# First norm of a four-layer graph kernel: steps in a written order, the mean taken away by a product, small weights loaded by GpSimd, idle products ahead of the input

## The chip, the cores and the metric

The kernel runs on one core of a Trainium2 chip. The metric is the device time of one execution in microseconds (us); lower is better. A core has a matrix engine (TensorE, "PE" in the profile, its weight loads are "PEld"), a vector engine (VectorE, DVE), a scalar engine (ScalarE, ACT), GpSimd (POOL) and a queue engine (SyncE, SP). Each works through its own instructions in the order in which they stand in its queue, and waits at an instruction until the semaphores that it needs have come. Transfers between memory and the on-chip buffers are DMAs; here they are issued by SP or by GpSimd.

## What is computed

`x` has 8 batches of 2048 nodes with 64 features. Four graph layers follow each other, and each has the form x = x + layer(relu(layernorm(x))):

```python
def _layernorm(x, axis=-1, eps=1e-5):
    m = jnp.mean(x, axis=axis, keepdims=True)
    v = jnp.var(x, axis=axis, keepdims=True)
    return (x - m) / jnp.sqrt(v + eps)
...
    h = jnp.maximum(_layernorm(x, axis=-1), 0.0)
    x = x + _L0_gnn_ref(h, L0_gnn_H, adj, 64, L0_gnn_W, L0_gnn_W_ind, ...)
```

The change lies in the first of these norms and in what is done beside it. Layer 0 uses the normed `h` in two ways. The first is a neighbourhood mean, `industry = einsum('nm,bmf->bnf', adj / deg, x @ W_ind)` (with x standing for h). The second is an attention over the members of 64 groups given by the 2048 x 64 matrix `H`. For that second part the kernel makes lists of (node, group) pairs from H.

## The kernel before

**Layout.** Two batches lie on the 128 partitions (2 x 64 features), so there are four pairs p of batches, and the 2048 nodes lie along the free dimension. The input comes transposed as `xT` [4, 128, 2048]. A half is 1024 nodes of one pair: 8 halves in all, each a 512 KB tile `x`, loaded in two parts of 256 KB. A mean over 64 features is a product with `avg`, a block-diagonal 128 x 128 matrix of 1/64, so that each feature's partition gets the mean of its own batch.

**The first stage (lines 882 to 912).** For each half: `mean = avg @ x` on TensorE (two products of 512 columns), `xc = x - mean` on DVE, `q = xc^2` on ScalarE, `var = avg @ q` on TensorE, `q = exp(-0.5 ln(var + eps))` on ScalarE in two instructions, and `hn = max(xc, 0) * q` on DVE. The helper `norm` (line 757) runs the steps of `norm_steps` (line 739) one after the other. Then eight products of 128 columns with `W_ind` give two tiles `py` (line 902); ScalarE copies them, rounded, to `Y[0]`, and DVE writes the rest `py - Y[0]` to `Y[1]` (lines 904 and 905).

**Beside the norm.** After the first pair `pairs` (line 833) makes the lists: it loads `H` as `M` (twice, line 844) and its transpose `MT` (line 847), counts with products against the triangle matrix `tri` (tiles `pr` and `pc`) and does DVE work that ends in `Q`, `mid`, `width` and the flags `bad`. After the second pair `weights` (line 813) and `layer1_weights` (line 684) load and multiply small weights, after the third `layer2_weights` (line 699). All these loads are issued by SP, 37 of them with `W_ind`, most of 64 x 64 or 64 x 1 elements.

**What sets the order.** The program text is not the order of the instructions. A scheduling layer places them on the engines, and a tile pool makes a new tile wait until the tile that had its place is released. Only instructions handed to `keep_in_program_order` keep the order of the text; the class `InOrder` (line 622) does that for all instructions of an engine that are issued through it, and `Kit.mm` (line 724) does it for products while `kit.strict` is set. In the first stage none of this was used. In that stage's PSUM pool `mean` has one place, `var` two and `yy` (py, pr, pc and the small products) two.

**What follows.** The second stage (line 914) streams the transposed adjacency in tiles `at` of 512 KB, six places, issued by GpSimd (line 932), and adds `Y` products into four sums `acc` (line 940); between these stand the products `ph` (line 982) and the other work of `members`. The `at` tiles and the sums lie where tiles of the first stage lay. SP also issues three copies of the input from memory to memory (`xd`, line 1241), and the loads `bw`, which wait for the first stage's places.

Of the kernel before, what the change touches and what calls it, by code (L numbers as in the profile page):

```python
# [16 lines left out]
P = 128  # L17
B, N, F = 8, 2048, 64
E = 64
# [615 lines left out]
class Kit:  # L635


    def __init__(self, tc, t, pool):
# [8 lines left out]
        for b2 in range(2):  # L647
            nc.vector.memset(self.avg[half(b2), half(b2)], 1.0 / F)
        self.eps = pool.tile([P, 1], FP, name="eps_f")
# [28 lines left out]
    def block_diag_in(self, w, src):  # L678
        self.nc.vector.memset(w, 0.0)
        for b2 in range(2):  # L680
            self.nc.sync.dma_start(out=w[half(b2), half(b2)], in_=src)
        return w

    def layer1_weights(self, pool, ps):
# [6 lines left out]
        for b2 in range(2):  # L691
            nc.sync.dma_start(out=a4[half(b2), b2 : b2 + 1], in_=t["L1_gnn_a"][F : 2 * F, :])
            nc.sync.dma_start(out=a4[half(b2), 2 + b2 : 3 + b2], in_=t["L1_gnn_a"][0:F, :])
        nc.vector.tensor_copy(self.W1x[:, 0:P], W)
        pw = ps.tile([P, 4], FP, tag="yy", name="pw1")
        nc.tensor.matmul(pw, WT, a4, start=True, stop=True)
        nc.vector.tensor_copy(self.W1x[:, P : P + 4], pw)

    def layer2_weights(self, pool, ps):

        nc, t, mm = self.nc, self.t, self.nc.tensor.matmul
# [4 lines left out]
        for dst, src in ((self.b1, "b1"), (self.b2c, "b2"), (self.ivc, "intervention_value")):  # L706
            for b2 in range(2):
                nc.sync.dma_start(out=dst[half(b2), :], in_=t[f"L2_gnn_{src}"])

        for dst, w in ((self.Wvc, self.W1v), (self.Wec, self.W1e)):  # L710
            pw = ps.tile([P, P], FP, tag="yy", name="pw2")
            mm(pw, W2n, w, start=True, stop=True)
            nc.vector.tensor_copy(dst, pw)
        pw = ps.tile([P, 1], FP, tag="yy", name="pwc")
        mm(pw, self.W1v, self.b2c, start=True, stop=True)
        nc.vector.tensor_add(self.b1c, pw, self.b1)
        r = pool.tile([P, P], FP, name="b2r")
        for h in range(2):
            nc.vector.tensor_scalar(r[:, half(h)], self.ones, self.b2c, None, op0=OP.mult)
        pw = ps.tile([P, P], FP, tag="yy", name="pwb")  # L720
        mm(pw, r, self.W1e, start=True, stop=True)
        nc.vector.tensor_copy(self.cb, pw)
# [33 lines left out]

    def norm(self, *tiles):
        for _ in self.norm_steps(*tiles):
            pass


def layer0(kit, hn, x1_dram, open_early, late_tile, between):
# [40 lines left out]
    with ExitStack() as sA:  # L803
# [9 lines left out]
        def weights(pool, ps):  # L813
# [5 lines left out]
            for b2 in range(2):  # L819
                nc.sync.dma_start(out=a2[half(b2), b2 : b2 + 1], in_=t["L0_gnn_a_node"])  # L820
                nc.sync.dma_start(out=a2[half(b2), 2 + b2 : 3 + b2], in_=t["L0_gnn_a_gn"])
            nc.sync.dma_start(out=a_ge, in_=t["L0_gnn_a_ge"].rearrange("f o -> o f").to_broadcast([P, F]))
            nc.sync.dma_start(out=fcb, in_=t["L0_gnn_fcb"])
            nc.sync.dma_start(out=av, in_=t["L0_gnn_av"])
            for b2 in range(2):
                nc.sync.dma_start(out=fcW[half(b2), :], in_=t["L0_gnn_fcW"])
            nc.vector.tensor_scalar(Av, ones, av, None, op0=OP.mult)
            nc.vector.tensor_copy(Wx[:, 0:P], W)
            pw = ps.tile([P, 4], FP, tag="yy", name="pw")
            mm(pw, WT, a2, start=True, stop=True)  # L830
            nc.vector.tensor_copy(Wx[:, P : P + 4], pw)

        def pairs(pool, ps):
# [4 lines left out]
            nc.vector.tensor_copy(slot, tmp)  # L838
# [1237 lines left out]
```

## Time and profile before

| | us |
|---|---|
| median of 3 runs | 2058.82 |
| lowest and highest of them | 2055.77, 2061.78 |
| the profiled execution: its own time | 2053.27 |
| its span in the profile | 2051.2 |
| first product of the first stage starts | 4.45 |
| first `acc` product of the second stage starts | 69.51 |
| end of the first eight `acc` and the first two `ph` products | 72.03 |
| mean granted TensorE clock over the span | 0.989 |

In the timeline each row has a start, a length, the engine, the line of the code, the operation and `out<-in`; in brackets stands how long the engine was idle before it and what ended that. SPq and POOL rows with `DMA_DIRECT2D` are the issue of a transfer, not the transfer. The releasers are inferred from semaphores. A product of fp32 data shows as two records of TensorE, so a count of x4 is two products. A granted clock of 1.00 is the full TensorE clock.

### The profile page before, as it was taken

The page shows a single profiled execution, that of the slowest core. Times are in us where ns is not written, and L with a number is a line of the kernel's source. Part 1 is how long each engine was busy: PE and PEld are TensorE (multiplying, and loading weights), DVE is VectorE, ACT ScalarE, POOL GpSimd, SP SyncE. Part 2 cuts the span into 40 slices and gives each one's busy share as a digit, 9 for nine tenths or more (in the row PEclk, how much of TensorE's full clock was granted, in tenths as well). Part 3 has the DMA queues.
Part 4 walks back from the last instruction along what each step waited for, and adds up shares of the span by engine and source line. Part 5 has one row for each costly group of instructions (what it writes and reads, how often), then busy time and mean ns, then how long its engine had stood idle before and what let it go on. Part 6 is the DMA issues. An engine that isn't in the chain of part 4 may idle for free.

```text
span 2051.2 us, 23618 instructions
## 1 busy us (share of the span) xinstructions
PE 1992.0 (97%) x9164; PEld 1153.7 (56%) x9164; DVE 1184.3 (58%) x1867; ACT 454.4 (22%) x859; POOL 291.4 (14%) x399
## 2 busy tenths in 40 slices
PE   7999899988999999999999999999999999999997
PEld 4777677623323232237774567665477745677653
DVE  6667399866888888873216552245622165522355
ACT  4321255474111111121120111211111211112100
POOL 0211187511000000000001110101100011101012
PEclk9999899999999999999999999999999999999998
DMA  6766173185011111204101012100021001121000
GB/s 172 207 192 189 59 249 113 36 228 107 27 47 37 47 32 42 52 11 111 57 21 29 24 42 67 47 15 24 23 68 57 21 22 30 42 67 46 8 15 12
DMA packets 84251, 138.17 MB, mean 67 GB/s; under 512 B 32752, under 2 KB 33008, under 8 KB 81456
## 3 DMA queue, kind: packets, MB, share of 16 engines
q1 hardware_dynamic: 65200, 83.86, 13.9%
q0 software_dynamic: 18928, 52.70, 10.5%
q8 instruction: 74, 1.21, 0.3%
q14 instruction: 49, 0.40, 0.1%
HBM read 102.64 MB, written 37.03 MB: 68 GB/s over the span
## 4 chain that ended last, share of the span: by engine, by line
PE 71%; issue 15%; POOL 4%; DVE 3%; DMA 3%; ACT 2%; SPq 0%; POOLq 0%; DVEq 0%; ACTq 0%
PE acc L726 28%; PE o L726 11%; PE dn L726 6%; PE u L726 6%; PE pd L726 3%; PE acc L940 3%; PE pgs L726 2%; PE var L726 2%; PE mean L726 2%; PE py L726 2%; POOL fold L1964 1%; DMA iv<-ind_dram 1%; PE pm L726 1%; POOL ot L1965 1%; PE ph L726 1%
## 5 line engine op out<-in xcount | busy, mean ns | idle before, releaser
L726 PE MATMUL acc<-aT,parts 128*128 128x512 f32 x1664 | 456.0, 419 | 0.0
L726 PEld LDWEIGHTS acc<-aT,parts 128*128 128x128 f32 x1664 | 307.8, 188 | 111.8 <-issue 49.4
L1952 DVE TENSOR_TENSOR pr<-u,embf 128x512 f32<-128x512 f32 x256 | 170.6, 687 | 139.0 <-PE u L726 132.3
L1571 DVE SCALAR_TENSOR_TENSOR pt<-R,wd,aT 128x1024 f32<-128x1024 f32 x192 | 236.3, 1277 | 18.4 <-PE dn L726 6.6
L726 PE MATMUL u<-W3f,y 64*128 64x512 f32 x1024 | 241.0, 589 | 0.0
L726 PE MATMUL o<-pt,hS 128*64 128x512 f32 x1024 | 236.4, 599 | 0.8 <-DVE pt L1571 0.6
L726 PEld LDWEIGHTS u<-W3f,y 64*128 64x128 f32 x1024 | 99.2, 187 | 120.6 <-issue 120.6
L726 PEld LDWEIGHTS o<-pt,hS 128*64 128x64 f32 x1024 | 68.0, 136 | 159.2 <-issue 150.2
L726 PE MATMUL u<-W3f,v 64*128 64x512 f32 x512 | 138.8, 619 | 0.0
L940 PE MATMUL acc<-at,Y 128*128 128x512 f32 x512 | 134.9, 408 | 1.7 <-DVE ev L949 1.7
L1964 POOL TENSOR_TENSOR fold<-fold 128x256 f32<-128x256 f32 x64 | 47.8, 747 | 548.2 <-DVE fold L1963 510.4
L726 PE MATMUL dn<-pt,vd 128*32 128x512 f32 x1024 | 123.1, 598 | 0.0
L1788 DVE TENSOR_TENSOR yb<-py,cb_f 128x512 f32<-128x512 f32 x32 | 22.1, 691 | 173.8 <-PE py L726 173.8
L940 PEld LDWEIGHTS acc<-at,Y 128*128 128x128 f32 x512 | 94.2, 192 | 24.8 <-issue 4.1
L726 PE MATMUL acc<-aTl,parts 128*128 128x512 f32 x384 | 103.1, 405 | 0.0
L1956 DVE TENSOR_TENSOR pr<-pr 128x512 f32<-128x512 f32 x128 | 88.1, 688 | 2.2
L1571 DVE SCALAR_TENSOR_TENSOR pt<-R,wd,aTl 128x1024 f32<-128x1024 f32 x64 | 79.8, 1281 | 11.4 <-PE dn L726 8.2
L726 PEld LDWEIGHTS acc<-aTl,parts 128*128 128x128 f32 x384 | 72.2, 188 | 21.5 <-issue 5.7
L1856 POOL TENSOR_TENSOR bq<-bq,xp 128x512 f32<-128x512 f32 x16 | 20.6, 1285 | 434.0 <-DVE xp L1854 395.1
L1938 ACT COPY xs<-px 128x128 f32<-128x128 f32 x64 | 17.1, 267 | 272.7 <-POOL ot L1966 210.2
L630 POOL TENSOR_TENSOR mix<-ex,wt 128x512 f32<-128x512 f32 x64 | 68.3, 1069 | 33.7 <-DVE ex L630 28.9
L726 PEld LDWEIGHTS dn<-pt,vd 128*32 128x32 f32 x1024 | 26.7, 108 | 80.8 <-issue 75.4
(322 smaller groups left out, 2723.0 us busy)
## 6 DMA issues: line engine op xcount, KB each, us to landing
at<-in_adjT POOLq DMA_DIRECT2D x32, 512.0 KB, 4.5
raw<-in_adjT SPq DMA_DIRECT2D x64, 256.0 KB, 3.3
aT<-in_adjT POOLq DMA_DIRECT2D x12, 1024.0 KB, 5.3
xp<-xd SPq DMA_DIRECT2D x45, 256.0 KB, 3.2
R<-r_dram SPq DMA_DIRECT2D x14, 512.0 KB, 3.7
hi_dram<-hi SPq DMA_DIRECT2D x16, 264.0 KB, 2.5
lo_dram<-lo SPq DMA_DIRECT2D x16, 264.0 KB, 3.4
hhi<-hi_dram POOLq DMA_DIRECT2D x16, 264.0 KB, 3.1
```

The costliest lines, as they stand in the source:

```text
L630: self.tc.keep_in_program_order(getattr(self.engine, name)(*args, **kw))
L726: one = self.nc.tensor.matmul(*args, **kw)
L940: mm(acc[p], Y[h][:, m, p, :], at[:, k, :], start=m + h == 0, stop=m == NT - 1 and h == 1)
L1571: nc.vector.scalar_tensor_tensor(pt, R[b2], wd[:, m, b2 : b2 + 1], aT[m][:, s].bitcast(FP), op0=OP.max, op1=OP.mult)
L1788: nc.vector.tensor_tensor(yb, py, bias[:, None, :].to_broadcast([P, 4, P]), op=OP.add)
L1856: nc.gpsimd.tensor_add(bq, bq, xp)
L1938: nc.scalar.copy(xs.rearrange("p h f -> p (h f)"), px)
L1952: nc.vector.tensor_tensor(a, u[h], emb[:, i, 8 * w : 8 * w + 8, None].to_broadcast([P, 8, F]), op=OP.mult)
L1956: nc.vector.tensor_add(pr[h], pr[h], a)
L1964: nc.gpsimd.tensor_add(fold[:, :, 0:2, :], fold[:, :, 0:2, :], fold[:, :, 2:4, :])
L1965: nc.gpsimd.tensor_add(ot, fold[:, :, 0, :], fold[:, :, 1, :])
```

## The change

- A matrix `cen = ident - avg` is made. `xc` is now the product `cen @ x` and stays in PSUM (two places); DVE's subtraction is gone, and Square and the last DVE instruction read PSUM. `var` has one place.
- The stage is written as steps: in step i TensorE gets var of half i-1, xc of half i and the map py of half i-2, with everything on TensorE, DVE and ScalarE kept in the text's order (`kit.strict`, `V`, `A`). The parts of `pairs` are spread over steps 0 to 7.
- The 37 small loads are issued by GpSimd. Their DVE copies stand in step 5, their products and the copies of these in step 8, in one PSUM tile.
- Six products of `avg` with `avg` go to a tile that nobody reads, ahead of the first x.
- On SP the order becomes: the first three x, MT, M twice, x of the fourth and fifth half, two of the three `xd` copies, the sixth x, the third copy, and the last two x.
- In the second stage the four sums of the first columns are allocated ahead of `pg` and `pd`. In the built program the first two `ph` products stand ahead of the first `acc` product; before they stood behind eight of them. They wait for the last `Y[1]` subtraction. From the first members of the second stage on, each engine's instructions stand in the same order as before.

```diff
+        self.cen = pool.tile([P, P], FP, name="cen_f")
+        nc.vector.tensor_sub(self.cen, self.ident, self.avg)
...
     def block_diag_in(self, w, src):
         self.nc.vector.memset(w, 0.0)
         for b2 in range(2):
-            self.nc.sync.dma_start(out=w[half(b2), half(b2)], in_=src)
+            self.nc.gpsimd.dma_start(out=w[half(b2), half(b2)], in_=src)
...
-    def layer2_weights(self, pool, ps):
+    def layer2_weights(self, pool, V, pw):
...
+                nc.gpsimd.dma_start(out=dst[half(b2), :], in_=t[f"L2_gnn_{src}"])
         r = pool.tile([P, P], FP, name="b2r")
+        yield
         for h in range(2):
-            nc.vector.tensor_scalar(r[:, half(h)], self.ones, self.b2c, None, op0=OP.mult)
+            V.tensor_scalar(r[:, half(h)], self.ones, self.b2c, None, op0=OP.mult)
+        yield
...
-            for p in range(NP):
-                for hf in range(2):
-                    s = cols(hf, HN)
-                    x = sb.tile([P, HN], FP, tag="x", name="x", bufs=3)
-                    for k in range(2):
-                        nc.sync.dma_start(out=x[:, cols(k)], in_=t["xT"][p, :, cols(2 * hf + k)])
-                    mean = ps.tile([P, HN], FP, tag="mean", name="mean", bufs=1)
-                    var = ps.tile([P, HN], FP, tag="var", name="var")
-                    xc = sb.tile([P, HN], FP, tag="xc", name="xc")
-                    q = sb.tile([P, HN], FP, tag="q", name="q")
-                    kit.norm(hn[p][:, s], x, mean, var, xc, q)
...
+            def centred(i):
+                x = xs.pop(i)
+                xc = xcs[i] = ps.tile([P, HN], FP, tag="xc", name="xc")
+                for k in range(2):
+                    kit.mm(xc[:, cols(k)], kit.cen, x[:, cols(k)], start=True, stop=True)
+
+            def squared(i):
+                q = qs[i] = sb.tile([P, HN], FP, tag="q", name="q")
+                A.activation(q, xcs[i], AF.Square)
...
+            def scaled(i):
+                p, hf = halves[i]
+                q = qs.pop(i)
+                A.activation(q, vs.pop(i), AF.Ln, bias=kit.eps)
+                A.activation(q, q, AF.Exp, scale=-0.5)
+                V.scalar_tensor_tensor(hn[p][:, cols(hf, HN)], xcs.pop(i), 0.0, q, op0=OP.max, op1=OP.mult)
...
+            def places():
+
+                all_ = ps.tile([P, 2 * CW], FP, tag="xc", name="pw")
+                at = iter(range(0, 2 * CW, P))
+                return lambda n: (lambda a: all_[:, a : a + n])(next(at))
+
+            fetched(0)
+            fetched(1)
+
+            idle = ps.tile([P, HN], FP, tag="var", name="idle", bufs=1)
+            for k in range(6):
+                nc.tensor.matmul(idle[:, 0:P], kit.avg, kit.avg, start=True, stop=True)
+            listed = pairs(pool, ps, V)
+            small = [f(pool, V, lambda n: pw(n)) for f in (weights, kit.layer1_weights, kit.layer2_weights)]
+            kit.strict = True
+            n = len(halves)
+            for i in range(n + 2):
+                if i + 2 < n:
+                    fetched(i + 2)
+                if i < 2:
+                    centred(i)
+                    squared(i)
+                if 0 < i <= n:
+                    spread_of(i - 1)
+                    scaled(i - 1)
+                if 1 < i < n:
+                    centred(i)
+                    squared(i)
+                if i < 4:
+
+                    next(listed)
+                if i > 1:
+                    mapped(i - 2)
+                    halved(i - 2)
+                if 3 < i < n:
+                    next(listed, None)
+                if i in (0, 5):
+                    for s in small:
+                        next(s)
+                if i == n:
+                    pw = places()
+                    for s in small:
+                        next(s)
+            kit.strict = False
...
+            sums = [ps.tile([P, CW], FP, tag=f"acc{p}", name=f"acc{p}") for p in range(NP)]
```

`fetched` issues the two loads of a half's x, `spread_of` the two variance products, `mapped` the eight map products and `halved` the copies to `Y[0]` and the subtractions to `Y[1]`. In `pairs` the comparison of MT stands in step 0, the `pr` products in step 1, their copies in step 2, `pc` in step 3, the sums of ranks in steps 4 and 5 (M in step 5), `Q` in step 6 and the rest in step 7.

## The prediction

> **What bounds the kernel now.** I read the busy shares first, then the stretches of the first stage, then its instructions by shape, its chain and its timeline.
>
> ```profile
> PE 1992.0 (97%) x9164; PEld 1153.7 (56%) x9164; DVE 1184.3 (58%) x1867; ACT 454.4 (22%) x859; POOL 291.4 (14%) x399
> ```
>
> TensorE is the bound over the span, so 65 us of the span can matter only where TensorE waits. Columns of the next view: stretch, its length, then busy time of each engine, granted clock, DMA share, GB/s.
>
> ```profile
> 4.40:26.30 21.90, 17.13 (x52) 8.38 (x52) 11.85 (x14) 8.67 (x10) 0.24 (x1) 1.00 0.72 155
> 26.30:40.30 14.00, 13.03 (x50) 7.42 (x50) 10.32 (x24) 6.07 (x6) 0.42 (x1) 0.88 0.30 87
> 40.30:69.50 29.20, 25.32 (x136) 17.52 (x137) 18.98 (x34) 18.76 (x24) 4.13 (x6) 1.00 0.73 234
> 69.50:200.00 130.50, 127.77 (x609) 101.47 (x608) 88.32 (x244) 26.74 (x103) 21.06 (x31) 1.00 0.66 196
> ```
>
> The norm stage runs from 4.45 to 69.51 us, 65.1 us, and TensorE idles 9.6 us of it and runs cold for part. The stage behind it is TensorE's (127.8 of 130.5 us). What the norm stage costs at its best is read from the shapes (count | busy, mean ns):
>
> ```profile
> L726 PE MATMUL mean<-x,avg_f 128*128 128x512 f32 x32 | 20.8, 779 | 7.0 <-DMA x<-in_xT 4.5 <-DVE xc L745 2.5
> L902 PE MATMUL py<-W_indf,hn 128*128 128x128 f32 x128 | 16.1, 279 | 3.5 <-DVE hn L754 2.0 <-DVE Y L905 1.3
> L726 PE MATMUL var<-q,avg_f 128*128 128x512 f32 x32 | 15.9, 615 | 2.0 <-ACT q L746 2.0
> L857 PE MATMUL pr<-tri,MT 64*128 64x64 f32 x32 | 3.8, 274 | 1.3 <-DVE Y L905 1.3
> ...
> L754 DVE SCALAR_TENSOR_TENSOR hn<-xc,q 128x1024 f32<-128x1024 f32 x8 | 9.8, 1223 | 6.0 <-ACT q L753 6.0
> L745 DVE TENSOR_TENSOR xc<-x,mean 128x1024 f32<-128x1024 f32 x8 | 9.7, 1217 | 8.9 <-PE mean L726 8.7
> ```
>
> One product shows as two records. Mean, variance and map (32+32+128 records) are 52.8 us of TensorE; the same work in long unbroken runs takes 0.43 us for a 512-wide record (the chain has var x4 in 1.73) and 1.78 for a half's 16 map records. So 8 halves need 8 x (1.73 + 1.73 + 1.78) = 41.9 us. The rest is waiting and cold clock. The chain shows how a half hangs on its own norm, and the timeline what the fill and the lists cost:
>
> ```profile
> 54.91 1.12 ACT q L752
> 56.06 1.06 ACT q L753
> 57.15 1.24 DVE hn L754
> ```
>
> ```profile
> 8.12 2.07 SPq L847 DMA_DIRECT2D MT<-in_HT  x1
> ...
> 26.35 3.78 PE L857 MATMUL pr<-tri,MT 64*128 64x64 f32 x32 [1.33 <-DVE Y L905]
> ...
> 30.06 3.49 PE L726 MATMUL mean<-x,avg_f 128*128 128x512 f32 x4
> 33.63 2.05 PE L726 MATMUL var<-q,avg_f 128*128 128x512 f32 x4
> 61.38 2.19 POOL L932 DMA_DIRECT2D at<-in_adjT  x3 [20.57 <-DVE hn L754]
> 69.51 2.07 PE L940 MATMUL acc<-at,Y 128*128 128x512 f32 x8
> ```
>
> ```profile
> x<-in_xT SPq DMA_DIRECT2D x16, 256.0 KB, 4.4
> MT<-in_HT SPq DMA_DIRECT2D x1, 512.0 KB, 8.4
> ```
>
> After the 3.8 us of small products (pr), four mean records take 3.49 us instead of 1.8: the clock had dropped. Also, the fifth and sixth x are issued only at 27.7 us and the last two at 38.6, because SP issues 21 and then 14 small weight loads ahead of them.
>
> **What the Trainium skill says.** "TensorE: Matmul & The Clock Gate", part 1 (the HAM clock gate): half rate until a free-running window of about 3.4 us has been busy. The trace agrees in kind: the first mean pair takes 3.75 us, the var pair at 13.09 takes 2.00. "VectorE: DVE Perf Modes", why PSUM operands drop a tier: fp32 from PSUM runs at 1x. Here that costs nothing, since two-input fp32 work takes 1.22 us from PSUM (xc) and 1.22 from SBUF (hn). "DMA: Bandwidth & Descriptors", issuing engines are not separate DMA queues: loads from GpSimd run on the same 16 engines and only save the other queue's issue time. The trace can't contradict it (DMA share 0.72 early on), and so I give no bandwidth gain.
>
> **The change part by part.**
>
> 1. *Mean by a product with ident - avg.* Product count stays: xc takes the place of mean, 1.73 us a half. Gone is DVE's subtraction, 8 x 1.22 = 9.7 us, and with it one hand-over between product and Square. Square and the last DVE step read PSUM: at most +0.05 us each (Ln from PSUM 1.11 against Square from SBUF 1.06). One extra DVE op makes the matrix (about 0.2 us), behind the memsets (end 3.58) and the slot copy (0.42): ready at 4.2-4.4, just ahead of x at 4.45. Free if so, else some tenths.
>
> 2. *The order.* Per step TensorE gets var(i-1), xc(i), py(i-2). From var's end: Ln 1.15, Exp 0.96, Square 1.08, so var to var through ScalarE is 1.73 + 3.3 = 5.0 us, under TensorE's 5.24. hn is done 5.3 us after var's start and needed at 8.9. DVE has 1.23 + 1.3 = 2.5 us a step, plus the lists (2.4 with M, 3.7 with Q and the reduce), whose surplus of about 1.5 us the 3.6 us of slack takes. I take 5.34 us a step.
>
> 3. *Fill.* x arrives at 4.45 as before. Six idle products fill 1.5 to about 4.1 us, so the clock rises one window earlier: xc0 ends at about 7.1 instead of 7.9 (between 6.2 and 7.9). xc1 to 8.85, var0 to 10.6. Then the small products pr wait for MT, which stands seventh on SP. Six x issues at 0.47 us put it at 3.6; with the 8.4 us that it took before it lands at 12.0, and its comparison (1.2, ahead of hn0 on DVE too) ends at 13.2. That wait is new in this place: 2.6 us of TensorE; if MT lands at 10, it is 0.6. pr 3.8 to 17.0; the clock drops behind it as before (+1.7); var1, xc2, py0 end at 23.9.
>
> 4. *Steady steps.* Five steps to the end of py5: 5 x 5.34 + 0.2 (pc) = 26.9, at 50.8.
>
> 5. *Drain.* var7 to 52.5. Ln, Exp, hn and hand-overs 3.65: py7 can start at 56.2. py6 (1.78) and the six small-weight products lie in that gap; they share one PSUM tile and alternate with DVE copies, about 2.0. py7 to 58.0. New here: the first two ph products stand ahead of the first acc, and their PSUM place waits for the last Y subtraction: copy 0.6 + subtraction 0.7 + 0.1, to 59.4. ph and the first eight acc 0.45 + 1.85: 61.7. Before, the same ten products were through at 72.03. **Saving 10.3 us**, 12.3 with MT early, about 8.5 with the clock low for longer.
>
> 6. *Small weights on GpSimd.* 37 loads in one queue: W_ind, then 35 more, each from the ninth on behind the completion of the load eight back. No row shows one this small. Nearest: hhi 0.55 us, issued 0.68 apart; "SBUF — State Buffer" (a bandwidth-pool intuition that's wrong) prices a load issued by GpSimd at about 620 ns alone and 3100 beside a DVE copy that holds the shared port. Low end 0.55, high end 1.1 us apart (landing up to 7.0 us early on, over eight in flight, gives 0.9). I take 0.75: the 35th, b2c, is issued at 2.5 + 34 x 0.75 = 28 and lands by 31. DVE waits for it in step 5 at about 41, and hn5, queued behind that wait, has 3.6 us more. So nothing, up to about 1.1-1.2 us each. Behind the weights on the same queue stand the adjT loads: the first now needs Q (about 46), the next three x7's product (49), 0.73 each plus landing 4.2 to 7.2, so the first is there at 53, the fourth at 58-59: at 59.9 acc begins. Its gain is that SP is free of 35 issues; priced in 2.
>
> 7. *xd copies* (three DRAM copies, landing 8.9 to 12.8 us before) move from behind the last x to before x5 and x6. By volume at about 200 GB/s M, x3 and x4 are in by 19 us, two copies (3.3 us each) by 26, x5 by 28: needed at 36. Hidden, with 8 us to spare; the rest likewise.
>
> Sum against the profiled execution: 2053.27 - 10.3 = 2043.0 (2.07 of it lies outside the span). That execution is 5.55 under the median shown, so the median becomes 2058.82 - 10.3 = **2048.5**. Behind the first members the engines' orders are the same in both programs, so I expect the gain to be carried to the end.
>
> **Rivals.**
>
> *A, the fill and transfers eat more.* MT, W_ind or x5 late by 3 to 6 us: each is a head-of-line wait on TensorE, and a gap that long brings the half clock (1.7 to 3.4 us). For it: DMA share 0.72 to 0.9 in the first 20 us. Against: before, TensorE waited only for the first x. Saving 2 to 7: about 2054.
>
> *B, the gain is given back.* The stage behind starts earlier but waits for adjT loads: DVE already waits 20.3 us for them from 70 to 200. For: the loads are now issued only 3 to 14 us ahead. Against: TensorE hardly waits there. About 2058.
>
> *C, slower: GpSimd's queue.* If its loads are p us apart, b2c lands at 5 + 34p and DVE, with hn5, the remaining steps and the first adjT load behind it, waits from 44.6 on. The 10.3 us are gone at 5 + 34p = 55, p = 1.47; at p = 1.7 the kernel is 8 us slower, 2067. For: in-order waits, the page's 3.1 us beside DVE copies. Against: DVE's port-holding work is only some 6 us of the first 40, so it adds 6/34 = 0.2 to p.
>
> **How the numbers follow.** Forecast 0.68, A 0.16, B 0.08, C 0.08. Forecast's own range 2044 to 2052; upward it takes in A, downward MT early and the spread of the three runs (3 us each way): 2041 to 2056. A measurement of this kernel can tell about 0.3%, 6.2 us, from no change. Faster by more than that: 0.68 and over half of A, 0.78; within: rest of A and B, 0.14; slower: C, 0.08.
>
> **What would show it.** The first acc near 59-60 us instead of 69.5; steps of 5.3 us with var, xc, py in turn; DVE's xc rows gone; pr waiting for MT's comparison at 10.6 to 13.2; a gap of 1 to 1.5 us ahead of ph; the last ivc issue on GpSimd before 35. Wrong if DVE's b2r waits for b2c, if xc waits for x, or if TensorE waits for the first adjT tiles.

## The result, and the profile after

| | before | after |
|---|---|---|
| median of 20 runs, us | 2057.32 | 2065.25 |
| lowest and highest of them | 2050.23, 2066.05 | 2058.48, 2071.32 |
| the profiled execution: its own time | 2053.27 | 2062.75 |
| its span | 2051.2 | 2061.0 |
| first `acc` product starts | 69.51 | 75.75 |
| end of the first eight `acc` and two `ph` products (the mark) | 72.03 | 77.7 |
| third `deg` product of the second stage starts | 194.04 | 203.65 |

The ratio after to before is 1.0042, with a 95% interval of 1.0031 to 1.0053: the changed kernel is slower, by some 9 us. The forecast was 10.3 us faster. In the profiled executions the forecast for this kernel was 2043.0 and 2062.75 came: 19.75 us are to be explained.

The busy totals of the changed kernel say little, as before: TensorE is the bound in both.

```profile
PE 1996.8 (97%) x9176; PEld 1160.9 (56%) x9176; DVE 1175.6 (57%) x1860; ACT 453.6 (22%) x859; POOL 310.8 (15%) x436
```

So the stretches of the first stage again, cut this time at the places that the prediction has numbers for: first product, var of the third half (var2), var of the last half (var7), the mark. Columns: stretch, its length, then busy time of PE, PEld, DVE, ACT and POOL, granted clock, DMA share, GB/s.

```profile
4.21:34.34 30.13, 21.43 (x70) 13.08 (x69) 5.48 (x9) 7.89 (x8) 15.92 (x31) 0.77 0.93 223
34.34:61.88 27.54, 26.68 (x125) 16.92 (x123) 19.12 (x27) 20.09 (x25) 3.36 (x7) 1.00 0.23 73
61.88:77.70 15.82, 11.46 (x63) 9.44 (x62) 9.45 (x33) 5.70 (x10) 3.58 (x5) 0.89 0.72 201
77.70:200.00 122.30, 116.00 (x554) 92.01 (x553) 77.21 (x225) 24.43 (x97) 19.71 (x29) 1.00 0.66 193
```

The second row is what the change promised: TensorE is busy for 26.7 of 27.5 us, at full clock, for five steps. In the rows above and below it TensorE stands idle (8.7 and 4.4 us) and the clock is low. Against the forecast:

| part | forecast | measured | difference |
|---|---|---|---|
| fill: var2 starts at | 23.9 | 34.34 | +10.4 |
| steps: var2 to var7 | 26.9 | 27.54 | +0.6 |
| drain: var7 to the mark | 10.9 | 15.82 | +4.9 |
| the mark to the end of the span, against before | 1979.2 | 1983.3 | +4.1 |

The sum is 20.0 (the time outside the span is 0.3 us shorter than before), and with that the difference is accounted for. Of the last row 3.9 us are there by the third `deg` product (126.0 us behind the mark instead of 122.0), 0.2 behind it. TensorE in the fill, in order of time:

```profile
10.23 1.12 PE L736 MATMUL xc<-x,cen_f 128*128 128x512 f32 x2 [2.96 <-DMA x<-in_xT]
11.19 3.19 PE L736 MATMUL var<-q,avg_f 128*128 128x512 f32 x4
17.94 6.65 PE L736 MATMUL pr<-tri,MT 64*128 64x64 f32 x32 [3.56 <-DVE MT L630]
24.52 3.78 PE L736 MATMUL var<-q,avg_f 128*128 128x512 f32 x4
28.09 2.18 PE L736 MATMUL xc<-x,cen_f 128*128 128x512 f32 x4
32.45 2.05 PE L736 MATMUL py<-W_indf,hn 128*128 128x128 f32 x16 [2.18 <-DVE rank L630]
34.34 1.88 PE L736 MATMUL var<-q,avg_f 128*128 128x512 f32 x4
```

Three waits: for the second half of the second x, for MT's comparison, and for the rank copies. Behind the first two the clock has dropped: pr takes 6.65 us for what took 3.78 before (granted clock 0.54 while it runs), the next var 3.78 instead of 1.88 (0.50). DVE had nothing to do from 4.8 us until MT was there, and the rank copies (the copies of pr) stand on it behind hn of the second half:

```profile
16.66 1.22 DVE L630 TENSOR_SCALAR MT<-MT 64x2048 f32<-64x2048 f32 x1 [11.84 <-DMA MT<-in_HT]
...
30.57 1.23 DVE L630 SCALAR_TENSOR_TENSOR hn<-xc,q 128x1024 f32<-128x1024 f32 x1 [11.56 <-ACT q L630]
31.71 1.28 DVE L630 COPY rank<-pr 128x512 f32<-128x512 f32 x2
```

The DMA view of the first 45 us (KB each, median us from issue to landing) shows what was slow:

```profile
x<-in_xT SPq DMA_DIRECT2D x16, 256.0 KB, 4.2
M<-in_L_gnn_H SPq DMA_DIRECT2D x2, 512.0 KB, 15.4
MT<-in_HT SPq DMA_DIRECT2D x1, 512.0 KB, 13.1
```

MT was issued at 3.54 as forecast (3.6) but took 13.1 us instead of 8.4. Right behind it on SP stands M, whose issue held SP until 16.2:

```profile
3.54 0.56 SPq L857 DMA_DIRECT2D MT<-in_HT  x1
4.14 12.08 SPq L868 DMA_DIRECT2D M<-in_L_gnn_H  x2
```

In the drain (from var7 on), TensorE waits in the middle of the small products and again ahead of `ph`. DVE's rows follow TensorE's: the copy that the second small product waits for stands behind hn of the last half and two subtractions.

```profile
65.77 0.28 PE L736 MATMUL pw<-a,W0Tf 128*128 128x4 f32 x2
68.67 0.39 PE L736 MATMUL pw<-a,W1Tf 128*128 128x4 f32 x2 [2.61 <-DVE W0x L630]
...
70.75 3.13 PE L736 MATMUL py<-W_indf,hn 128*128 128x128 f32 x16
75.28 0.72 PE L1073 MATMUL ph<-W0x,hn 128*128 128x132 f32 x4 [1.40 <-DVE Y L630]
75.75 3.92 PE L1031 MATMUL acc<-at,Y 128*128 128x512 f32 x16
```

```profile
66.12 1.23 DVE L630 SCALAR_TENSOR_TENSOR hn<-xc,q 128x1024 f32<-128x1024 f32 x1 [0.71 <-ACT q L630]
67.26 1.28 DVE L630 TENSOR_TENSOR Y<-py,Y 128x512 fp32r<-128x512 f32 x2
68.46 0.15 DVE L630 COPY W0x<-pw 128x4 f32<-128x4 f32 x1
```

And in the second stage there is a wait that the kernel before did not have. GpSimd's queue, then DVE, then TensorE:

```profile
86.14 0.56 POOL L805 DMA_DIRECT2D hhi<-hi_dram  x1 [5.45 <-DMA hi_dram<-hi]
86.69 0.71 POOL L1023 DMA_DIRECT2D at<-in_adjT  x1
```

```profile
93.54 1.22 DVE L1036 TENSOR_TENSOR ds<-ds,at 128x1024 fp32r<-128x1024 f32 x1 [4.49 <-DMA at<-in_adjT]
```

```profile
95.24 0.69 PE L1073 MATMUL ph<-W0x,hn 128*128 128x132 f32 x4 [3.44 <-DVE lo L1066]
```

The eighth load of `at` stands behind a load of the features, `hhi`, which waits for a store (hi_dram). In the kernel before, the eighth `at` stood ahead of that load:

```profile
78.77 0.71 POOL L932 DMA_DIRECT2D at<-in_adjT  x1 [3.86 <-PE acc L940]
79.84 0.56 POOL L799 DMA_DIRECT2D hhi<-hi_dram  x1 [0.36 <-DMA hi_dram<-hi]
```

The sentence in the section on the change, that every engine has the same order from the first members of the second stage on, is wrong here: on GpSimd two neighbours have changed places, `hhi` and the eighth `at`, and so have the next `hhi` and the ninth `at`.

### The profile page after: what moved, and what is told of

Same layout as the page of the kernel before. It is cut to its first block, busy times and chain, and to the rows that moved or that the text cites. A ratio compares the mean times of both kernels' runs of the same rounds, so it can differ in the third digit from the quotient of the medians.

```text
span 2061.0 us, 23638 instructions
## 1 busy us (share of the span) xinstructions
PE 1996.8 (97%) x9176; PEld 1160.9 (56%) x9176; DVE 1175.6 (57%) x1860; ACT 453.6 (22%) x859; POOL 310.8 (15%) x436
## 3 DMA queue, kind: packets, MB, share of 16 engines
q0 software_dynamic: 20112, 53.10, 10.5%
## 4 chain that ended last, share of the span: by engine, by line
PE 71%; issue 16%; POOL 4%; DVE 3%; DMA 3%; ACT 2%; SPq 0%; POOLq 0%; DVEq 0%; ACTq 0%
PE acc L736 28%; PE o L736 11%; PE dn L736 6%; PE u L736 6%; PE pd L736 3%; PE pgs L736 3%; PE py L736 2%; PE var L736 2%; PE mean L736 2%; POOL fold L2055 1%; PE acc L1031 1%; PE pm L736 1%; POOL ot L2056 1%; PE ph L736 1%; POOL ot L2057 1%
## 5 line engine op out<-in xcount | busy, mean ns | idle before, releaser
L630 POOL TENSOR_TENSOR mix<-ex,wt 128x512 f32<-128x512 f32 x64 | 67.8, 1062 | 34.2 <-DVE ex L630 28.9
L736 PEld LDWEIGHTS dn<-pt,vd 128*32 128x32 f32 x1024 | 26.7, 108 | 80.8 <-issue 74.6
```

The lines of the kernel that those rows point to most:

```text
L630: self.tc.keep_in_program_order(getattr(self.engine, name)(*args, **kw))
L736: one = self.nc.tensor.matmul(*args, **kw)
```

## The experiments

How to compare them: what follows the third `deg` takes 1855 to 1868 us in the spans of the profiled executions of these kernels, with no relation to the edits that could be seen. The runs of one kernel spread by as much (before: 2050 to 2066). So one span tells little, and each experiment is read by its marks in the trace (var2, first `acc`, third `deg`) and by the ratio of its runs to those of the kernel before on the same chip. Only the ratios of mt_first, drain, best1 and best2 have intervals that lie clear of the changed kernel's; what the other runs show rests on the marks of one profiled execution each. The five kernels with SP's queue as in the changed kernel (after, w_late, one_idle, drain, at_first) spread by 1.4 us at var2, which tells how exact such a mark is.

| kernel | MT: us to landing | var2 | first acc | third deg | ratio to before, interval |
|---|---|---|---|---|---|
| before | 8.4 | | 69.5 | 194.0 | 1 |
| after | 13.1 | 34.3 | 75.7 | 203.7 | 1.0042, 1.0031 to 1.0053 |
| m_late | 8.8 | 30.5 | 70.3 | 197.8 | 1.0039, 1.0025 to 1.0053 |
| w_late | 12.5 | 34.2 | 75.6 | 204.2 | 1.0040, 1.0025 to 1.0055 |
| mw_late | 9.6 | 29.5 | 72.4 | 203.3 | 1.0037, 1.0019 to 1.0054 |
| mt_first | 7.0 | 25.5 | 66.9 | 195.1 | 1.0011, 0.9996 to 1.0027 |
| warm | 11.2 | 32.9 | 72.6 | 200.0 | 1.0033, 1.0014 to 1.0051 |
| warm20 | 10.5 | 30.6 | 72.0 | 201.9 | 1.0031, 1.0019 to 1.0042 |
| one_idle | 12.4 | 34.1 | 75.5 | 203.5 | 1.0039, 1.0021 to 1.0057 |
| drain | 11.5 | 32.9 | 68.4 | 194.9 | 0.9996, 0.9982 to 1.0011 |
| at_first | 12.0 | 33.6 | 73.4 | 197.4 | 1.0025, 1.0005 to 1.0046 |
| before_g | 9.1 | | 72.1 | 197.1 | 1.0029, 1.0018 to 1.0040 |
| best1 | 10.4 | 29.2 | 64.7 | 188.7 | 0.9955, 0.9936 to 0.9973 |
| best2 | 7.3 | 23.9 | 59.4 | 183.3 | 0.9930, 0.9911 to 0.9948 |

**Why MT is late: M behind it, or the small loads (m_late, w_late, mw_late).**

```diff
-            for h in range(2):
-                nc.sync.dma_start(out=M[:, :, h, :], in_=t["L0_gnn_H"].rearrange("(t p) e -> p t e", p=P))
             yield
...
             V.tensor_copy(past, pc)
+            for h in range(2):
+                S.dma_start(out=M[:, :, h, :], in_=t["L0_gnn_H"].rearrange("(t p) e -> p t e", p=P))
             yield
```

> The changed kernel with M's two loads moved on SP's queue from behind MT to behind the x of the sixth half; nothing else moves. Theory T1 (M's two loads, 12 us on SP, take the DMA engines from x and MT and hold x3 back): MT lands at about 12 instead of 16.6 us, DVE's wait for it falls from 11.8 to about 7 us, the small products pr start near 13, the clock stays up, and var of the third half starts at 26 to 28 instead of 34.3 us; the first eight acc and the ph ahead of them are through at about 70 instead of 77.7, and the time is about 7 us under that of the changed kernel, near 2057. Theory T2 (the small loads of GpSimd slow MT): MT still lands after 15.5, var of the third half starts after 32, time near 2064.

```diff
-                nc.gpsimd.dma_start(out=a2[half(b2), b2 : b2 + 1], in_=t["L0_gnn_a_node"])
+                kit.G.dma_start(out=a2[half(b2), b2 : b2 + 1], in_=t["L0_gnn_a_node"])
...
-                if i in (0, 5):
+                if i in (2, 5):
```

> The changed kernel with the 35 small loads of GpSimd (all but W_ind) held back until DVE has done its work of the third step; SP's loads as they are. T2 (small loads, 4 to 256 bytes a piece, share the DMA engines with x and MT from 3 to 20 us): MT lands at about 12, pr near 13, var of the third half at 26 to 28 instead of 34.3, time near 2057. T1 (M is the cause): MT lands after 15.5, var of the third half after 32, time near 2064. Either theory: the last of the small loads is issued some 20 us later, near 60, and if it is later than 62 the step before the last waits for it and gives some of the gain back.

> Both edits: M behind the x of the sixth half, small loads behind the third step. T1 and T2 agree that MT then lands by 12 us, as the prediction had it. If they share the cause, this is better than either alone: var of the third half at about 24 (the forecast's figure) against 28 to 31 in each alone. If the cause is neither (MT alone, 32 kB rows on 64 partitions, simply takes 12 us beside six x), MT lands after 15 here too and var of the third half starts after 32.

With M late DVE's wait falls to 7.56 us and pr starts at 13.66:

```profile
4.14 1.42 SPq L1332 DMA_DIRECT2D xd<-in_xT  x2
...
13.66 7.09 PE L736 MATMUL pr<-tri,MT 64*128 64x64 f32 x32 [3.32 <-DVE MT L630]
```

With the small loads late nothing moves (wait 11.23, pr at 17.33), and with both late MT takes 9.6 us, no less than with M late alone. (MT's rows are 8 KB, 2048 numbers, and not 32 kB as the expectation has it.) The theory that the small loads take the bandwidth falls: they land late themselves, but they are not what delays MT. M is part of it: in the five kernels that have M right behind MT on SP, MT took 11.5 to 13.1 us (mean 12.3), in the five with M late and MT seventh 8.8 to 11.2 (mean 10.1). But more moved than M: in the built program two of the `xd` copies stand in M's place, issued at 4.14, so how soon MT would land with nothing behind it is not shown. And m_late gave only 3.9 us at var2, not 6 to 8, for pr was as slow as before (7.09 us) and the rank copies were waited for again. Of the 5.4 us at the first acc the ratio shows 0.6, with an interval of some 3 us either way; mw_late lost its gain behind the first acc (at `deg` it is level with the changed kernel). There `ph` waited 3.35 us, as in the changed kernel (3.44), but then ran at half clock, and so did the eight acc behind it: 1.22 and 3.77 us instead of 0.69 and 2.08. One edit of the fill was not the whole story.

**Where MT stands on SP (mt_first).**

```diff
             fetched(0)
+            nc.sync.dma_start(out=MT, in_=t["HT"])
             fetched(1)
...
-            nc.sync.dma_start(out=MT, in_=t["HT"])
             V.tensor_scalar(MT, MT, 0.0, None, op0=OP.is_gt)
```

> The changed kernel with one thing moved: MT's load stands third on SP, ahead of the x of the second half, instead of seventh. Every engine's order but SP's is the same. Theory (MT is late because six x stand ahead of it and share the DMA engines with it): MT lands at 10 to 11 instead of 15.3 to 16.7 us, the second half's x some 2 us later at 9 to 10, pr starts at 12 instead of 18, and var of the third half at 27 to 29 instead of 34.3; first acc 5 us sooner, near 70. Rival (M and the small loads behind it hold MT up wherever it is issued): MT lands after 13.5, gain under 3 us at var of the third half.

This one load, moved by four places on one queue, gives 8.9 us at var2 and at the first acc, and 0.31% of the time (1.0042 to 1.0011, about 6.4 us). TensorE's fill in its timeline:

```profile
9.02 1.98 PE L736 MATMUL xc<-x,cen_f 128*128 128x512 f32 x4 [1.58 <-DMA x<-in_xT]
10.84 1.88 PE L736 MATMUL var<-q,avg_f 128*128 128x512 f32 x4
12.65 3.78 PE L736 MATMUL pr<-tri,MT 64*128 64x64 f32 x32
16.36 3.09 PE L736 MATMUL var<-q,avg_f 128*128 128x512 f32 x4
...
23.59 2.05 PE L736 MATMUL py<-W_indf,hn 128*128 128x128 f32 x16 [1.84 <-DVE rank L630]
25.48 1.88 PE L736 MATMUL var<-q,avg_f 128*128 128x512 f32 x4
```

The reader should compare the row of pr with the changed kernel's: without a wait ahead of it, it is at full clock (granted 1.00). M still comes behind the x here, issued 2.9 us after MT instead of 0.6, and best2, with MT in this place and M late, has 7.3: with MT third, M's absence brings nothing more. How much of the gain comes from the four loads of x that no longer stand ahead of MT, and how much from the greater distance to M, this run does not separate.

A sum of bytes shows what to expect. The DMA engines moved 181 GB/s in the first 10 us of the changed kernel and 149 in the next 10. At these rates (an estimate) three x and MT, 2.1 MB, are through at about 12 us, which is what the prediction had, and with M's two loads of 0.52 MB, issued from 4.1 us on, at about 19. MT came in between, at 16.6, when some 2.8 MB had been moved: the loads right behind it took a part of the rate. In mt_first the first x and MT are 1.05 MB; MT was there at 8.6 us, when at the mean rate of 198 GB/s some 1.7 MB had been moved.

**Is it the cold clock (warm, warm20, one_idle).** Idle products between var of the first half and pr:

```diff
                 pr = ps.tile([P, 8, E], FP, tag="yy", name="pr")
+                for _ in range(8 if g == 0 else 0):
+                    kit.mm(pr[:, 0:2, :].rearrange("p a b -> p (a b)"), kit.avg, kit.avg, start=True, stop=True)
```

> M late as in the run of that name, and eight idle 128-column products on TensorE between var of the first half and pr, in the place where TensorE waits for MT. Theory: the wait lets the clock drop, and pr (7.1 us instead of 3.8), the next var (3.8 instead of 1.9) and xc are slow for that reason alone: with the gap filled pr takes about 3.8, var of the third half starts at 25 to 26 instead of 30.5 us, the first acc at 65 to 66 instead of 70.3. Rival: pr (64-row, 64-wide products) does not count as busy enough for the clock, as it was followed by slow products before the change as well: pr may run fast but var behind it is slow, and half of the gain is left. Eight products too many cost up to 1 us.

Eight took 1.95 us and ended 3.1 us before MT was there, which by chance was late in this execution (11.2 us). So TensorE was idle after all, pr took 7.09 us, and the run could not tell the theories apart. With 20:

> The run warm, but with 20 idle products ahead of pr (4.9 us at 0.24 each) instead of eight, which ended 3 us before MT was there, so that TensorE was idle again and nothing of the clock could be seen. Theory: with the gap closed pr takes 3.8 us instead of 7.1 and the var behind it under 2.5 instead of 3.8; var of the third half starts at 26 to 28. Rival (the small products pr themselves let the clock drop, as in the kernel before): pr starts fast, but var behind it still takes 3 us or more, and the gain at var of the third half is under 3 us against 30.5.

```profile
11.78 4.63 PE L736 MATMUL pr<-avg_f 128*128 128x128 f32 x40
16.34 4.47 PE L736 MATMUL pr<-tri,MT 64*128 64x64 f32 x32
20.74 3.78 PE L736 MATMUL var<-q,avg_f 128*128 128x512 f32 x4
```

Both are partly right. Without a gap pr takes 4.47 instead of 7.1 us, so the gap did slow it; but var behind pr is slow all the same, as in mt_first and in the kernel before. The idle products also ran 0.9 us past MT's comparison, and var2 came out where m_late had it: they mend the clock and cost their own time.

```diff
-            for k in range(6):
+            for k in range(1):
                 nc.tensor.matmul(idle[:, 0:P], kit.avg, kit.avg, start=True, stop=True)
```

> The changed kernel with one idle product at the start instead of six. The prediction gave the six about 0.8 us at the first xc. Theory: in the changed kernel the second half's x and then MT are late anyway, so the first acc stays within 1 us of 75.7 and the time within 2 us of the changed kernel's. Rival: the cold clock of the first products pushes var of the first half, Ln, Exp and hn behind MT: 2 us or more.

First acc 75.5 against 75.7, ratio 1.0039 against 1.0042: the six idle products of the change bring nothing, since what follows waits for MT. The two xc took 5.57 us from 4.10 on, and var of the first half started at 9.50. In the two kernels with six idle products in which xc did not wait for x either, it started at 8.75 (at_first) and 8.46 (m_late), so they are worth 0.8 to 1.0 us where nothing else waits, near the 0.8 that the prediction gave them.

**The drain.** All six small products ahead of the DVE copies:

```diff
             kit.mm(p, WT, a2, start=True, stop=True)
+            yield
             V.tensor_copy(Wx[:, P : P + 4], p)
...
                 if i == n:
                     pw = places()
-                    for s in small:
-                        next(s)
+                    for _ in range(2):
+                        for s in small:
+                            next(s)
```

> The changed kernel with the six products of the small weights issued first and the DVE copies of their results behind all of them (before, the second product stood behind DVE's copy of the first result, which stands behind hn and the last subtractions). Theory: TensorE's wait of 2.61 us ahead of pw<-a,W1Tf goes; the products are done by about 67 instead of 70.7 and the last map py can start with hn of the last half, 2 to 3 us sooner; with no long gap the clock stays up for it (2.0 instead of 3.1 us); first acc 4 us sooner after var of the third half (37.5 instead of 41.4 us). Rival: hn of the last half is itself only there 6 us after the last var starts, so the gap moves to py and the gain is under 1 us.

```profile
64.36 0.28 PE L738 MATMUL pw<-a,W0Tf 128*128 128x4 f32 x2
...
65.47 0.28 PE L738 MATMUL pw<-b2c_f,W1v_f 128*128 128x1 f32 x2
66.59 2.05 PE L738 MATMUL py<-W_indf,hn 128*128 128x128 f32 x16 [0.83 <-DVE Y L630]
68.40 2.07 PE L1035 MATMUL acc<-at,Y 128*128 128x512 f32 x8
```

First acc 35.5 us after var2 instead of 41.4: 5.9 us gained, more than expected (5.4 at the mark, which has `ph` in it on both sides). Two things beyond the edit came with it. In the built program `ph` stands behind the first eight acc again, so its wait of 1.40 us is gone; and on GpSimd the eighth `at` stands ahead of `hhi` again, which is the order of the kernel before. GpSimd in this run:

```profile
77.65 0.71 POOL L1027 DMA_DIRECT2D at<-in_adjT  x1 [3.86 <-PE acc L1035]
78.72 0.56 POOL L807 DMA_DIRECT2D hhi<-hi_dram  x1 [0.36 <-DMA hi_dram<-hi]
```

So this edit undoes the drain and the second stage at once: at the third `deg` it is 8.7 us ahead of the changed kernel (1.4 from a fill that happened to be shorter, 5.9 from the drain, the rest behind it), and 0.46% in the ratio, which brings it level with the kernel before although its fill is as bad as ever (var2 at 32.9).

**The second stage alone (at_first).**

```diff
-        nc.gpsimd.dma_start(out=hi, in_=hi_dram[i].bitcast(FR))
-        nc.gpsimd.dma_start(out=lo, in_=lo_dram[i].bitcast(FR))
+        kit.late.dma_start(out=hi, in_=hi_dram[i].bitcast(FR))
+        kit.late.dma_start(out=lo, in_=lo_dram[i].bitcast(FR))
...
-                    nc.gpsimd.dma_start(
+                    kit.late.dma_start(
```

> The changed kernel with the loads of at and of the two halves of the features put on GpSimd's queue in the order of the text, so that the eighth at load no longer stands behind a load that waits for the store of the features. Theory: DVE's wait of 4.5 us for at at 93.5 us goes, and with it TensorE's 3.4 us ahead of ph at 95.2; what lies before 80 us stays as it is (mark near 77.7); the time falls by 3 to 4 us to about 2061. Rival: the wait for the features' store is on the way to later work anyway, and what was waited for at 93 is waited for some us later: under 1 us of gain at the end.

The wait of 3.44 us ahead of `ph` is gone (TensorE is busy for all of 90 to 100 us, 6.56 in the changed kernel). The third `deg` comes 6.3 us sooner; 2.3 of this was there at the first acc already (the first xc and MT were a little earlier in this execution), so 4.0 belong to the edit, as the table above has it. All kernels together say the same. From the first acc to the third `deg` it takes 127.4 to 130.9 us in the eight that have the `hhi` load ahead of the eighth `at`, 124.0 in the three with these loads in the text's order (at_first, best1, best2), and 124.5 in the kernel before, 125.1 in before_g and 126.5 in drain, which have the eighth `at` first too. The ratio fell by 0.0017 with an interval that does not exclude nothing.

**One part of the change alone (before_g).** The kernel before, with the small loads issued by GpSimd (the edit moves `W_ind` too, so 37 loads and not the 35 of the expectation):

```diff
         for b2 in range(2):
-            self.nc.sync.dma_start(out=w[half(b2), half(b2)], in_=src)
+            self.nc.gpsimd.dma_start(out=w[half(b2), half(b2)], in_=src)
```

> The kernel before with one part of the change alone: its 35 small weight loads on GpSimd's queue instead of SP's. Theory: the part helps SP (x of the fifth half issued at about 20 instead of 27.7 us, of the last at 32 instead of 38.6) but TensorE was not waiting for those x, so the first acc moves by less than 2 us from 69.5 and the time by less than 3. Rival: the small loads take 3 to 12 us each to land on that queue while SP's loads run, as in the changed kernel, and what waits for them (the small products, at 46 to 64 us) or for the first at loads behind them comes later: first acc 2 us or more later, time 4 us or more over the kernel before.

The rival's numbers hold: 2.6 us at the first acc, 0.29% in the ratio. The wait is another than the ones that it named, and comes much earlier. DVE and TensorE in its timeline:

```profile
17.82 0.23 DVE L828 COPY W0x<-W0f 128x128 f32<-128x128 f32 x1 [2.69 <-DMA W0f<-in_L_gnn_W]
17.97 1.22 DVE L754 SCALAR_TENSOR_TENSOR hn<-xc,q 128x1024 f32<-128x1024 f32 x1
```

```profile
19.24 3.78 PE L902 MATMUL py<-W_indf,hn 128*128 128x128 f32 x16 [3.76 <-DVE hn L754]
```

The small loads are now early in the program's order, the copy of W0f is placed ahead of the first hn on DVE, and W0f takes 7.4 us to land; in the kernel before, py waited 1.37 us here. That this wait is all of the 2.6 us was not tried. The queue that issues was freed; who waits for the load was moved too.

**All mends together.** best1 has M late, eight idle products, the rank copies ahead of hn of the second half, the products ahead of their copies, and the `at` loads in order. best2 leaves these eight idle products out (the six at the start stay), and has MT third on SP and the `xd` copies behind the last x:

```diff
                 if 0 < i <= n:
                     spread_of(i - 1)
+                    if i == 2:
+                        next(listed)
                     scaled(i - 1)
...
-            nc.sync.dma_start(out=x1_dram[p], in_=t["xT"][p])
+            kit.S.dma_start(out=x1_dram[p], in_=t["xT"][p])
```

> All that is thought to be wrong mended at once: M late, the gap ahead of pr filled with idle products, the rank copies ahead of hn of the second half on DVE, the six small products ahead of their copies, and the at loads in text order on GpSimd. By the marks: fill 9 to 10 us better than in the changed kernel, drain 3, second stage 3: the first acc at 62 to 63 us instead of 75.7, the loads of at from then on 13 to 15 us ahead of the changed kernel's and 5 to 6 ahead of those of the kernel before; time near 2051, ratio to before about 0.997. Rival: what is gained ahead of 200 us is lost between 200 and 410 us, where TensorE's clock drops behind its waits (a late start had cost nothing there and an early start gains nothing): then the third deg still starts near 190 but the time is over 2056, not faster than before.

> The run best1 without its idle products, with MT third on SP and the DRAM copies xd behind the last x. Theory: pr finds MT there at 11 to 12 us, so TensorE has no gap and no cold clock in the fill: var of the third half at 23 to 24 instead of 29.2, first acc at 58 to 60 instead of 64.7, time 4 to 6 us under best1's, near 2043. Rival: the later x of the second half costs as much as MT's earlier landing gains: first acc after 63, time as best1's, near 2048.

best1 is faster than both kernels (2047.59 us against the 2051 expected, 0.9955), though its fill is not good: MT took 10.4 us again and the first acc came at 64.7, not at 62 to 63. best2 is the best of all, 2042.46 us over six runs, 0.70% under the kernel before (interval 0.52 to 0.89%). Its stretches, cut at the same four places:

```profile
4.22:23.90 19.68, 17.91 (x70) 9.89 (x69) 5.49 (x8) 7.76 (x8) 15.34 (x31) 0.91 0.64 155
23.90:51.44 27.54, 26.68 (x125) 16.92 (x123) 19.21 (x27) 20.10 (x26) 3.64 (x7) 1.00 0.40 94
51.44:61.91 10.47, 9.54 (x63) 7.80 (x62) 9.16 (x30) 5.14 (x8) 3.58 (x5) 1.00 0.94 263
```

Its var2 starts at 23.90, where the prediction has 23.9, and its ten products are through at 61.9, where it has 61.7. That the fill agrees so well is in part luck:

```profile
9.44 2.08 PE L740 MATMUL xc<-x,cen_f 128*128 128x512 f32 x4 [1.77 <-DMA x<-in_xT]
...
13.17 3.78 PE L740 MATMUL pr<-tri,MT 64*128 64x64 f32 x32
```

pr starts at 13.17 where the prediction has 13.2, but not because of MT, which was there at 9.0: the second x, now behind MT, was late, and var of the first half ran until 13.2 instead of 10.6. The drain is not the forecast one either: here the ten products begin with acc, and the wait of 1.4 us ahead of `ph` is gone.

## Why the prediction was wrong

The failed step is step 3, the fill: "Six x issues at 0.47 us put it at 3.6; with the 8.4 us that it took before it lands at 12.0". The issue time was right (3.54), the landing was not: 16.6. The 8.4 us were carried over from another place. In the kernel before MT was issued at 8.12, with M ahead of it; here it was issued at 3.54, behind six x and 0.6 us ahead of M. This one load took 7.0 to 13.1 us in these kernels, by what was under way around it. A term that step 3 put at nothing is the loads right behind MT: the bytes ahead of it alone give, by the estimate above, the forecast's 12 us. With M gone from there, but copies in its place, it took 8.8 to 11.2 us; issued third, 7.0 and 7.3, and the fill came to 1.6 us (mt_first) or 0.0 us (best2, in part by luck) from the forecast. How the 4.6 us by which MT was late divide between M, the x ahead and whatever else is not settled.

The 10.4 us of the fill add up from the rows. pr starts 4.7 us late (17.94 instead of 13.2), behind MT. It then takes 2.9 us more than the 3.8 forecast, for in the wait the clock had dropped. Behind it 2.8 us more are lost, 2.18 of them in a second term that step 3 left out: py of the first half needs the PSUM places of pr, which are free only after the rank copies, and these stand behind hn of the second half on DVE (a wait of 2.18 us in the changed kernel, 1.84 in mt_first, none in best1 and best2, which have the copies ahead of that hn).

- *Step 1, the product for the mean:* right. DVE's subtraction is gone, xc starts at 4.21, Square and the last DVE step cost what they did (1.01 and 1.22 us).
- *Step 2, the order, and step 4, the steps:* right. var to var is 5.25 us after the first (5.34 forecast), 27.54 us for five steps with the first (26.9); the first took 6.57, since py waited 0.86 us for DVE's copy of `pc` (0.2 forecast for `pc`).
- *Step 5, the drain:* wrong by 4.9 us. "About 2.0" for the six small products is the term: they took 5.0, from 65.77 to 70.75. The products and the copies alternate, and the first copy stands on DVE behind hn of the last half and two subtractions, so TensorE waits 2.61 us for a copy of 0.15. The last py starts 8.9 us after var7 instead of 5.4, and, as the clock had dropped behind the wait, it took 3.13 us instead of 1.8: together 4.8 of the 4.9. ph then waited 1.40, as forecast. With the products first they take 1.4 us (drain: 64.36 to 65.75).
- *Step 6, small weights:* hidden, as forecast. Most issues took 0.52 to 0.58 us each and b2c was issued at 39.1, 1.08 us apart on average, inside the bounds but not at the 0.75 taken: the ninth load was issued only when the first had landed (11.26), and so on, and they took up to 12.6 us to land. In best2, where step 5 comes at 45 us, b2c was in time too. The 3100 ns for a load of GpSimd's beside a DVE copy, from the Trainium skill ("SBUF — State Buffer", a bandwidth-pool intuition that's wrong), no run here shows: no issue of a small load took over 0.79 us in the changed kernel. But before_g shows that this part is not free where a DVE copy is placed early; in the changed kernel the written order (copies in step 5) protects it.
- *Step 7, xd:* the copies were hidden in the changed kernel, though not as reckoned: x of the fourth and fifth half were not in by 19 us, but only issued from 16.3 on, when M had let SP go. When M was moved away they moved up to 4.1 us and took its place on the DMA engines, which may be why the five kernels with M late still took 8.8 to 11.2 us for MT; this was not tried apart.
- *The sum's last sentence*, that the gain is carried since "the engines' orders are the same": wrong by 3.9 us up to the third `deg`, for GpSimd's order was not. at_first gets 4.0 us back with that order alone.

Rival A (fill and transfers eat more) named the mechanism, but priced it at 3 to 6 us with 2 to 7 us of saving left; it was over 10, and it did not stand alone. Rivals B and C did not come: TensorE did not wait for adjT tiles because of their late issue, but because of a swap in the queue; and GpSimd's loads held up nobody in this kernel.

Not settled: m_late is 5.9 us ahead at the third `deg`, and its ratio shows 0.6 us; the interval of each ratio is 2 to 4 us either way, and what made the rest of that kernel slower, if anything did, was not looked for. Where the clock of a profiled execution is low behind 200 us (0.81 in the stretch from 200 to 300 us in m_late, drain, warm and one_idle, 0.90 and 0.91 in the two kernels) is open too; no edit lies in that stretch.

## What to carry to other kernels

Before a load is moved or loads are placed ahead of it, count the bytes that are under way on all queues, those ahead of it and those issued right behind it, and divide by the rate that the profile shows. Here the landing lay between the two sums; the old landing time held only for the old place. A written order is only as good as its shortest hand-over: a product that waits for a copy on an in-order engine waits for all that stands ahead of the copy, so issue the products of a group first and their copies after. And when an edit leaves the scheduler any freedom, compare the built queues all the way into the next stage, the DMA queues too: here two neighbours that changed places cost 4 us.

## What the runs showed of the hardware

- How long a small load takes went with the traffic at that moment more than with the queue that issued it: W0f (16 KB) on GpSimd landed in 12.6 us in the changed kernel, in 7.0 in best2 and in 2.6 when issued after the first steps (w_late); from SP in the kernel before it took 7.0.
- SP's own time for an issue differs as much: M's two loads held SP for 12.08 us in the changed kernel, from 4.14 on, against 3.76 in the kernel before and 3.93 in m_late, so that the x behind them were issued at 16.3 instead of 6.9.
- The DMA engines were as busy with M in flight as without it, but moved less: share 1.06 and 149 GB/s from 10 to 20 us in the changed kernel, 0.98 and 351 in m_late, where copies from memory to memory took M's place. M is read in pieces of 256 bytes, 64 numbers: in these 10 us 4319 of 4471 packets are under 512 bytes in the changed kernel, 287 of 854 in m_late. How much of the difference is due to the small pieces, and how much to the way that copies within memory are counted, was not tried.
- pr, 16 products of 64 rows and 64 columns, leaves a low clock behind it even when nothing waits: var behind it took 3.09 us (mt_first), 3.41 (best2) and 3.78 (warm20), at a granted clock of 0.62, 0.56 and 0.50, against 1.88 in later steps. pr itself ran at 1.00 in mt_first and best2.
